# Four layers of a graph network: other buffers and another order at both ends of the program

## The chip, the core and the metric

The kernel runs on one core of a Trainium2 chip. The core has five engines that run their own instruction streams and wait for each other by semaphores: TensorE (PE, matrix products), VectorE (DVE), ScalarE (ACT), GpSimd (POOL) and SyncE (SP, which here only issues DMAs). The metric is the device time of one execution in microseconds (us); lower is better. Times are given as the median of several runs. A profile is one further execution, recorded instruction by instruction; its span is the time from the first to the last recorded instruction.

## What is computed

The input is 128 graphs of 128 nodes with 256 features, and one adjacency matrix for each. Four layers follow each other; every one adds its result to its input and normalises the sum over the features.

```python
x = layernorm(x + L0(x, adj, a0..a3))        # attention: scores (x * a_k) @ x.T picked by adj == k+1,
                                             # leaky_relu, softmax, @ x
x = layernorm(x + L1(x, adj, W_msg, W_upd))  # mean of the neighbours' messages, + x @ W_upd + bias, relu
x = layernorm(x + L2(x, adj, weight, w_ih, w_hh, b_ih, b_hh))
# L2: three times   m = h @ weight[i];  aggr = A.T @ m;  h = GRU(aggr, h)
#     r, z = sigmoid(...); n = tanh(i_n + r * h_n); h = (1 - z) * n + z * h
x = layernorm(x + L3(x, adj, W, a))          # Wh = x @ W; e_ij = leaky_relu(f_i + f_j), f from Wh @ a
                                             # masked softmax over j, @ Wh, elu
```

## The kernel before, in words

**Groups and stages.** Four graphs make a group; there are 32 groups, `NG`. For each group the program records the operations of `loading`, `layer0`, `layer1`, `gru` (three steps, step0 to step2) and `layer3`. Several groups are under way at a time: while one is in its GRU steps, the next ones load and run layers 0 and 1, and the previous one runs layer 3. The last group's layer 3 is done in two halves of two graphs.

**A planner sets the order.** Nothing is issued while a layer's function runs. The functions record operations; `spread` and `paced` (line 334) give each a nominal time, from the table `TIMES`, the distance of groups `PERIOD` (line 294) and corrections for the first six and the last six groups, `HEAD` and `TAIL`. At the end a loop goes through an estimate of the engines: at each turn it takes the engine that is free first, and of that engine's ready operations the one with the lowest nominal time. So the constants decide the order of each engine's stream, and a change of them moves instructions everywhere. The stream itself is fixed when the program is built; on the chip each engine runs its own in order. Every operation is recorded through one helper, so the profile gives line 229 for all of them; tiles tell them apart.

**Buffers.** `tile_of(tag, shape, bufs)` (line 136) asks for one of `bufs` buffers of that tag. A new tile of a tag has to wait until an old one of the same tag has been read for the last time. The tags that matter: `x_blocks`, `x_in`, `adj_in` (a group's input), `alpha0` (layer 0's scores), `xs`, `xT` (products' operands in layer 0), `x1T` (layer 0's result, turned), `rT` (the residual of the GRU layer, turned), `xc` (its result), `t_r`, `t_i`, `t_z`, `q` (parts of the gates), `e`, `alpha3`, `xd` (layer 3). PSUM has four banks named `ps` and four named `gate`.

**Turning a matrix.** [...]states are turned several times per group. The ordinary way is `turn` and `back`: DVE transposes blocks of 32x32 into `z`, SP writes `z` to DRAM (`way_...`) and reads it back in the other order with four DMAs. For the first group, and for the result of the last group's last step, `turned_quick` is used: PE transposes four blocks into a PSUM bank and ACT copies it out.

**The GRU step.** `sums` (line 735) forms four sums `t_h` of the state's quarters (on POOL) and four `t_m` of the aggregate (on DVE), so that each gate takes seven half products in place of eight. `gate` issues them in turn with evictions between. `update` (line 823) forms the new state in `hT`, turns it (`way_h`, `hn`), and `split` (on DVE) makes the three bf16 parts, `hn` and two `rest`, that the next step's aggregate needs as exact operands: products with `a_ne`. The next step's gates need the new `hT` only, the aggregate needs `hn` and `rest`.

**Layer 3.** `layer3` (line 883) computes the statistics of `xc`, products of `rT` with `w3x`, evicts them as `wh` scaled by the inverse deviation on ACT, and brings f_j of all nodes into every partition: DVE turns a column into `z_f`, SP writes it to DRAM (`way_f`) and reads it back broadcast into `e`. Then masks, softmax, products with `wh`, ELU (two ReLUs, Exp), the last `normalise` (line 538) and the store.

**Weights.** `weights` (line 370) loads them from ACT's and SP's queues, turns `w_ih`, `w_hh` and `weight` on PE, and multiplies `weight` by `w_ih` (the 24 products each with `wh,hT` and `xc,hT`) so that step i needs one matrix `c_gi`. It runs in the same planner beside the first groups' loads and layer 0.

Of the kernel before, what the change touches and what calls it, by code (L numbers as in the profile page):

```python
# [18 lines left out]
def kernel(  # L19
# [71 lines left out]
    class View:  # L91
# [38 lines left out]
        def real(self):  # L130
# [3 lines left out]
            return ap  # L134

    def tile_of(tag, shape, bufs=1, dtype=F32, pool=work):
        buf = Buf(pool, list(shape), dtype, tag, bufs)
        return View(buf, list(shape), [(0, n) for n in shape])
# [98 lines left out]
    PAIRS = ("tensor_tensor", "tensor_add", "tensor_sub", "tensor_mul", "scalar_tensor_tensor", "copy_predicated")  # L237
    SERVED = {"e": 3.5, "x1T": 0.9, "adj_in": 1.6, "x_in": 1.6, "xc": 1.5, "way_x2": 1.5, "way_f": 0.2}

# [43 lines left out]
    def sp_cost(op, n, out, ins, pointers, sums):  # L283
# [9 lines left out]

    PERIOD = 82.02493
    EAGER, RUSH = 5.3026, 1.3855
    HOP, PE_HOP, SLACK, DMA_SLACK = 0.0942, 0.0830, 0.2614, 0.8331
    STAGES = ("loading", "layer0", "layer1", "step0", "step1", "step2", "layer3")
    TIMES = {
        "loading": ((-247.5491, -194.0561), (-143.2722, -216.6135),),
        "layer0": ((-168.5251, -107.0951),),  # L300
        "layer1": ((-55.2002, 2.6695),),
        "step0": ((-4.9084, 19.3012), (-1.4435, 21.3222), (15.5190, 41.5941),),
        "step1": ((50.8640, 70.9820), (56.8513, 77.3906), (67.7313, 96.3666),),
        "step2": ((107.7073, 126.4989), (122.9713, 129.9877), (118.3791, 151.2368),),
        "layer3": ((179.8434, 241.7064),),
    }
    HEAD = (
        (-126.155, 5.128, -69.803, -21.348, -13.669, -8.174, -16.851),
        (80.207, 34.377, 38.524, -17.547, 20.300, -9.109, -5.064),
        (7.408, -12.202, 25.610, 5.632, -5.558, 8.108, 7.059),  # L310
        (-65.918, 41.138, 4.487, 5.072, -12.230, 11.065, -14.228),
        (-137.367, -1.144, -2.252, -1.129, -3.189, 2.308, 8.092),
        (153.242, -9.402, 11.531, 0.561, -10.941, 4.205, 0.017),
    )
    TAIL = (
        (27.368, -6.179, -9.810, -20.906, -9.678, 2.832, 10.136),
        (-37.995, 0.038, 5.644, -1.049, -11.456, -16.322, -4.360),
        (57.786, 10.690, 2.358, -3.167, -6.918, -6.271, -6.896),
        (-15.895, -28.941, -7.001, -17.741, -17.830, -3.775, -5.809),
        (-97.576, -12.624, -18.430, -10.462, 23.529, 14.526, 53.629),  # L320
        (97.074, 26.443, 18.854, 20.435, 13.060, 47.535, 73.872),
    )
# [11 lines left out]
    def paced(stage, part, g):  # L334

        start, end = TIMES[stage][part]
        at = g * PERIOD
        if g < len(HEAD):
            at += HEAD[g][STAGES.index(stage)]
        elif g >= NG - len(TAIL):  # L340
            at += TAIL[g - NG][STAGES.index(stage)]
        spread(at + start, at + end, stage[:4] == "step")

    def row(v, n):
# [25 lines left out]
    def weights():  # L370

        POOL.memset(neg_half, -0.5)
        nats, wnat = [], []
        for src, tag, bufs in ((w_ih, "hT", 9), (w_hh, "rest", 4)):
# [9 lines left out]
        spread(-215.1, -206.9)  # L384
        for k, a in enumerate((a0, a1, a2, a3)):
            SP.dma_start(out=acol[:, k, :], in_=a.rearrange("(c p) -> p c", p=P))
        spread(-182.0, -173.8)
        SP.dma_start(out=w_um[:, :, :D], in_=w_upd.rearrange("(c p) u -> p c u", p=P))
# [6 lines left out]
        SP.dma_start(out=arow, in_=row(a_att, 2 * D))  # L395
        spread(-165.5, -124.1)

# [7 lines left out]
        for n, dst in enumerate((w_ihT, [w_hhT[:, c] for c in range(KC)])):  # L405
            for g in range(NGC // 2):
                nat = nats[n * NGC // 2 + g]
                ps = bank()
                with PE:
                    for c in range(KC):  # L410
                        for e in range(2):
                            PE.transpose(
                                ps[:, (2 * c + e) * P : (2 * c + e + 1) * P], nat[:, e, c * P : (c + 1) * P], ident
                            )
                for c in range(KC):
                    out_of(dst[c][:, 2 * g * P : (2 * g + 2) * P], ps[:, 2 * c * P : 2 * (c + 1) * P])


        for i in range(NL):
            wT = tile_of("hT", [P, KC, D], 9)  # L420
            ps = bank()
# [7 lines left out]
            for d in range(KC):  # L429
                for n0, n1 in ((0, 512), (512, 3 * D)):  # L430
                    ps = bank()
                    with PE:
                        for e in range(KC):
                            PE.matmul(
                                ps[:, : n1 - n0],
                                wT[:, e, d * P : (d + 1) * P],
                                w_ihT[e][:, n0:n1],
                                start=(e == 0),
                                stop=(e == KC - 1),
                            )  # L440
                    out_of(c_gi[:, i, d, n0:n1], ps[:, : n1 - n0])


# [35 lines left out]
        for c in range(KC):  # L479
            DVE.tensor_sub(w3x[:, c, :], w3x[:, c, :], ps[:, : 2 + D])  # L480
        spread(-157.2, -16.5)

# [55 lines left out]
    def normalise(res, shift, rstd, quick):  # L538

        for b in range(res.shape[1]):  # L540
            if quick and b % 2 == 0:
                DVE.tensor_scalar(
# [51 lines left out]
    def layer0(g, s):  # L594
# [39 lines left out]
        for h in range(G // 2):  # L634
# [5 lines left out]
            for j in range(2):  # L640
# [4 lines left out]
                )  # L645
        normalise(res, *statistics(res, "0"), g == 0)
        s.x1T = tile_of("x1T", [P, G, KC, N])
# [11 lines left out]
    def layer1(g, s):  # L659
# [17 lines left out]
        for b in range(G):  # L677
# [14 lines left out]
        normalise(res, *statistics(res, "1"), g == 0)  # L692

        s.hT, s.parts, s.ways = [], [], []
        for c in range(KC):
            t = tile_of("hT", [P, T], 9)
# [12 lines left out]
    def gru(g, s):  # L709
# [5 lines left out]
        def step(i, hT, parts):  # L715
# [107 lines left out]
            def update(c, z, n, d):  # L823

                DVE.scalar_tensor_tensor(d, z, 1.0, d, op0=OP.add, op1=OP.mult)
                new[c] = n if last_step else tile_of("hT", [P, T], 9)
                DVE.scalar_tensor_tensor(new[c], d, 0.5, n, op0=OP.mult, op1=OP.add)
                if last_step:
                    turning[c] = s.x3[:, :, c * P : (c + 1) * P]
                else:  # L830
                    turning[c] = tile_of("hn", [P, G, P], 3)
                if last_step and g == NG - 1:
                    turned_quick(turning[c], [new[c][:, b * N : (b + 1) * N] for b in range(G)])
# [16 lines left out]
            if last_step:  # L850
# [32 lines left out]
    def layer3(g, s, first, last):  # L883
# [48 lines left out]
        pT, rinv = softmax(alpha, three, end, tile)  # L932
        normalise(x3, shift, rstd, end)

# [3 lines left out]
        for h in range(n // 2):  # L938
# [167 lines left out]
```

## Time and profile before

| | us |
|---|---|
| median of 3 runs | 2739.55 (2733.42 to 2739.82) |
| the profiled execution's own time | 2739.76 |
| its span | 2737.9 |
| PE busy with products | 2675.7 |
| DVE busy | 2207.6 |
| ACT busy | 1798.1 |
| POOL busy | 1619.3 |

The profile counts an engine as busy while one of its instructions runs. PE's weight loads are counted apart (PEld). An f32 product is two records, a bf16 product one. "PEclk" is the clock that PE was granted, as a share of full speed. Lines of the timeline read: start, duration, engine, operation, tiles written and read, count, and in brackets how long the engine was idle before and who released it.

### The profile page before, as it was taken

The numbers are of one execution on the slowest core, as the hardware profiler recorded it, in microseconds if no ns is written. First come the engines' busy times: TensorE is split into PE (matmuls) and PEld (weight loads), VectorE is DVE, ScalarE is ACT, GpSimd is POOL, SyncE is SP. The second block draws the span as 40 slices with busy tenths as digits, with TensorE's granted clock in tenths as the row PEclk, the third lists the DMA queues.
The fourth block names the chain that finished last, engine by engine and source line by source line (L and its number), as shares of the span: only waits on it lengthen the run. The fifth ranks groups of instructions, "written<-read, shape, count | busy, mean of one in ns | idle before, by whom it ended". The sixth has DMA issues, their size and how long they took to land.

```text
span 2737.9 us, 45131 instructions
## 1 busy us (share of the span) xinstructions
PE 2675.7 (98%) x14332; PEld 2232.2 (82%) x14332; DVE 2207.6 (81%) x5044; ACT 1798.1 (66%) x4336; POOL 1619.3 (59%) x1546
## 2 busy tenths in 40 slices
PE   8999999999999999999999999999999999999996
PEld 5788888788888888888888888888888888888784
DVE  5777788888788888888888788888888878888775
ACT  4557666666776666776666776666776666666665
POOL 4555656555666555666555667555656555666542
PEclk9999999999999999999999999999999999999997
DMA  5445555465555555555555555555555556553532
GB/s 121 102 80 116 96 118 115 91 120 103 111 110 111 106 119 100 113 111 110 108 117 106 107 111 110 110 115 108 105 113 108 106 104 117 100 110 81 104 70 51
DMA packets 1385662, 288.38 MB, mean 105 GB/s; under 512 B 1139408, under 2 KB 1385296, under 8 KB 1385424
## 3 DMA queue, kind: packets, MB, share of 16 engines
q1 hardware_dynamic: 1382976, 283.13, 52.1%
q10 hardware_dynamic: 2448, 2.36, 0.3%
q8 instruction: 115, 1.88, 0.3%
q14 instruction: 123, 1.01, 0.1%
HBM read 168.96 MB, written 116.38 MB: 104 GB/s over the span
## 4 chain that ended last, share of the span: by engine, by line
PE 84%; DVE 8%; ACT 4%; DMA 1%; issue 1%; SPq 1%; POOL 1%; DVEq 0%; POOLq 0%; ACTq 0%
PE gate L229 57%; PE ps L229 27%; DVE t_d L229 1%; DVE hT L229 1%; DVE z L229 1%; DVE t_m L229 1%; SPq L229 1%; DVE rest L229 1%; ACT xc L229 1%; ACT t_z L229 0%; ACT xs L229 0%; DVE t_z L229 0%; DVE xb L229 0%; DMA hn<-way_h 0%; ACT alpha L229 0%
## 5 line engine op out<-in xcount | busy, mean ns | idle before, releaser
L229 POOL TENSOR_TENSOR t_r<-t_r,t_i 128x512 f32<-128x512 f32 x186 | 248.7, 1349 | 242.4 <-DVE t_r L229 118.6
L229 PE MATMUL gate<-t_h,w_hhT 128*128 128x256 f32 x1152 | 343.5, 384 | 8.3 <-ACT t_z L229 6.7
L229 PE MATMUL gate<-t_h,w_sh 128*128 128x256 f32 x1152 | 338.4, 383 | 7.0 <-ACT q L229 4.0
L229 PE MATMUL gate<-t_m,c_gi 128*128 128x256 f32 x1152 | 341.4, 379 | 0.0
L229 PE MATMUL gate<-agT,c_gi 128*128 128x256 f32 x1152 | 338.8, 382 | 0.6 <-DVE q L229 0.3
L229 PE MATMUL gate<-t_m,w_sm 128*128 128x256 f32 x1152 | 339.1, 379 | 0.2 <-ACT t_i L229 0.2
L229 PE MATMUL gate<-hT,w_hhT 128*128 128x256 f32 x1152 | 333.0, 383 | 2.6 <-DVE mv L229 1.6
L229 POOL TENSOR_TENSOR t_d<-hT,t_n 128x512 f32<-128x512 f32 x192 | 257.4, 1349 | 43.3 <-ACT t_n L229 43.0
L229 PEld LDWEIGHTS gate<-t_h,w_sh 128*128 128x128 f32 x1152 | 210.2, 190 | 70.0 <-issue 18.4
L229 POOL MEMSET alpha<- 128x512 f32 x64 | 33.4, 522 | 392.7 <-DVE z L229 349.9
L229 PEld LDWEIGHTS ps<-xs,xT 128*128 128x128 f32 x2048 | 250.4, 194 | 11.5 <-ACT xs L229 2.5
L229 PE MATMUL ps<-xs,xT 128*128 128x128 f32 x2048 | 254.1, 278 | 3.2 <-DVE xa L229 1.4
L229 PEld LDWEIGHTS gate<-t_h,w_hhT 128*128 128x128 f32 x1152 | 207.1, 190 | 56.2 <-issue 16.3
L229 PEld LDWEIGHTS gate<-hT,w_hhT 128*128 128x128 f32 x1152 | 215.3, 191 | 43.4 <-issue 12.3
L229 POOL TENSOR_TENSOR rstd<-rstd,neg_half 128x4 f32<-128x4 f32 (+1 forms) x128 | 157.0, 1227 | 147.9 <-DVE rstd L229 147.0
L229 PEld LDWEIGHTS gate<-t_m,w_sm 128*128 128x128 f32 x1152 | 218.1, 190 | 32.2 <-issue 1.2
L229 PEld LDWEIGHTS gate<-agT,c_gi 128*128 128x128 f32 x1152 | 216.5, 190 | 32.3 <-DVE q L229 2.3
L229 PEld LDWEIGHTS gate<-t_m,c_gi 128*128 128x128 f32 x1152 | 217.3, 190 | 30.6 <-issue 0.7
L229 PE MATMUL ps<-w_um,x1T 128*128 128x512 f32 x512 | 240.6, 593 | 0.4 <-ACT x1T L229 0.2
L229 ACT ACTIVATE q<-gate,bhn 128x256 f32<-128x256 f32 x384 | 182.1, 474 | 83.8 <-PE gate L229 78.9
L229 POOL TENSOR_SCALAR mk<-a_f 128x512 uint8<-128x512 f32 x128 | 200.9, 1576 | 27.8 <-DVE alpha L229 18.5
L229 ACT COPY t_r<-gate 128x256 f32<-128x256 f32 x288 | 106.6, 370 | 153.8 <-PE gate L229 153.2
(185 smaller groups left out, 6746.3 us busy)
## 6 DMA issues: line engine op xcount, KB each, us to landing
way<-z SPq DMA_DIRECT2D x188, 256.0 KB, 2.5
way_h<-z SPq DMA_DIRECT2D x128, 256.0 KB, 2.4
hn<-way_h SPq DMA_DIRECT2D x512, 64.0 KB, 2.3
x_blocks<-in_x_dram SPq DMA_DIRECT2D x256, 64.0 KB, 2.4
x_in<-in_x_dram SPq DMA_DIRECT2D x32, 512.0 KB, 4.3
rT<-way SPq DMA_DIRECT2D x256, 64.0 KB, 2.3
way_p<-z SPq DMA_DIRECT2D x62, 256.0 KB, 2.5
probT<-way_p SPq DMA_DIRECT2D x248, 64.0 KB, 2.5
```

Of the source, the lines that this page charges most:

```text
L229: getattr(self.engine, name)(*[a.real() if isinstance(a, View) else a for a in args], **{k: a.real() if isinstance(a, View) else a for k, ...
```

## The change

Seven edits, and new constants for the planner:

- `lent`: for some groups a tag is replaced by another tag whose buffers are idle then. Group 1 takes its inputs and its layer 0 in buffers of layer 3 and of the gates. Groups 30 and 31 take `rT`, `xc`, `q`, `t_r`, `t_i` and `t_z` of the GRU in buffers of loads and of layers 0 and 1.
- The last group's new states after step1 too are turned by `turned_quick` (before: after step2 alone).
- `t_h` is formed on DVE in two steps: group 0's step0 and the last group's step2.
- In the last group's layer 3 DVE takes two of the four ReLUs of each half.
- The last `normalise` of group 30 goes to DVE as a whole.
- `way_f` is written as one row of 512 and read back as one.
- The weights' stages are given their times in seven parts by `early`, with constants of their own, so their loads and their work stand elsewhere among the first groups' operations. `hT` has 8 buffers instead of 9.

```diff
+    lent = {}
+
     def tile_of(tag, shape, bufs=1, dtype=F32, pool=work):
+        tag, bufs = lent.get(tag, (tag, bufs))
         buf = Buf(pool, list(shape), dtype, tag, bufs)
...
-    SERVED = {"e": 3.5, "x1T": 0.9, "adj_in": 1.6, "x_in": 1.6, "xc": 1.5, "way_x2": 1.5, "way_f": 0.2}
+    SERVED = {"e": 1.3, "x1T": 0.9, "adj_in": 1.6, "x_in": 1.6, "xc": 1.5, "way_x2": 1.5, "way_f": 0.2}
...
-    PERIOD = 82.02493
+    PERIOD = 81.73028
...
+        "weights": ((-80.6792, -53.8982), (-234.5413, -66.3537), (-85.3398, -177.0436), (-97.3878, -222.0278), (-90.3491, -54.1657), (-171.8955, -44.6841), (-116.1849, 18.7475),),
...
+    def early(part):
+
+        spread(*TIMES["weights"][part])
...
-            if quick and b % 2 == 0:
+            if b % 2 < quick:
...
-                if last_step and g == NG - 1:
+                if g == NG - 1 and i > 0:
                     turned_quick(turning[c], [new[c][:, b * N : (b + 1) * N] for b in range(G)])
...
-            of_h = sums(POOL, hT, w_hhT, w_sh, hT, "t_h")
+            of_h = sums(DVE if g + i in (0, NG + 1) else POOL, hT, w_hhT, w_sh, hT, "t_h")
...
-            way = tile_of("way_f", [P, 32], 4, F32, dram)
-            SP.dma_start(out=way, in_=z)
-            SP.dma_start(out=f, in_=way.rearrange("(m r) c -> r m c", [8, 16, 32], r=8)[0].partition_broadcast(P))
+            way = tile_of("way_f", [16, 32], 4, F32, dram)
+            SP.dma_start(out=way, in_=z.rearrange("(m r) c -> r m c", [8, 16, 32], r=8)[0])
+            SP.dma_start(out=f, in_=way.partition_broadcast(P))
...
-                ACT.activation(res[:, b, :], pb, AF.Relu, scale=rinv[:, b : b + 1])
-                ACT.activation(pb, pb, AF.Relu, scale=ninv[:, b : b + 1])
+                for to, by in ((res[:, b, :], rinv), (pb, ninv)):
+                    if end and j == 0:
+                        DVE.tensor_scalar(to, pb, by[:, b : b + 1], 0.0, op0=OP.mult, op1=OP.max)
+                    else:
+                        ACT.activation(to, pb, AF.Relu, scale=by[:, b : b + 1])
...
-        normalise(res, *statistics(res, three), end)
+        normalise(res, *statistics(res, three), 2 if g == NG - 2 else int(end))
...
+    LENT = {
+        1: {
+            "x_blocks": ("t_z", 1), "x_in": ("t_i", 1), "adj_in": ("alpha3", 1), "alpha0": ("e", 1),
+            "probT_0": ("probT_3", 1), "x1T": ("xd", 1), "xs": ("rT", 2),
+        },
+        NG - 2: {"xc": ("xa", 2), "rT": ("xT", 2)},
+        NG - 1: {
+            "q": ("x_in", 1), "t_r": ("x_blocks", 1), "t_i": ("xb", 2), "t_z": ("xb", 2),
+            "xc": ("xa", 2), "rT": ("xs", 2),
+        },
+    }
...
+        lent.update(LENT.get(g, {}) if g == 1 else {})
         loading(g, s)
         layer0(g, s)
...
+        lent.clear()
+        lent.update(LENT.get(g, {}) if g > 1 else {})
         gru(g, s)
```

The remaining lines of the diff are the other constants of `TIMES`, `HEAD` and `TAIL`, the calls of `early` in `weights`, and `int(...)` around the third argument of `normalise`. In PE's stream the change adds eight transposes of 128x128, all in group 31, and removes nothing; DVE's grows by 14 instructions, SP's loses ten DMAs. The order of the streams differs throughout: between groups 13 and 22 both kernels repeat one pattern of products per group, and the two patterns are not the same.

More of the change, by code (lines that the diff above doesn't have):

```diff
@@ L291 @@
     engines = (PE, DVE, ACT, POOL, SP)
-    PERIOD = 82.02493
-    EAGER, RUSH = 5.3026, 1.3855
-    HOP, PE_HOP, SLACK, DMA_SLACK = 0.0942, 0.0830, 0.2614, 0.8331
+    PERIOD = 81.73028
+    EAGER, RUSH = 4.9441, 1.5064
+    HOP, PE_HOP, SLACK, DMA_SLACK = 0.0975, 0.1022, 0.2622, 0.8243
     STAGES = ("loading", "layer0", "layer1", "step0", "step1", "step2", "layer3")
     TIMES = {
[L299 to L305, printed above, removed]
+        "weights": ((-80.6792, -53.8982), (-234.5413, -66.3537), (-85.3398, -177.0436), (-97.3878, -222.0278), (-90.3491, -54.1657), (-171.8955, -44.6841), (-116.1849, 18.7475),),
+        "loading": ((-270.5681, -253.3431), (-73.2168, -291.6634),),
+        "layer0": ((-167.8607, -107.2636),),
+        "layer1": ((-55.0836, 1.9826),),
+        "step0": ((-0.0120, 6.9518), (0.2402, 27.6105), (15.5871, 41.1624),),
+        "step1": ((50.3003, 61.9650), (57.0688, 76.7749), (63.5441, 96.9672),),
+        "step2": ((105.0974, 124.9583), (122.1936, 130.3892), (118.2271, 151.0122),),
+        "layer3": ((180.2686, 241.7351),),
@@ L306 @@
     }
     HEAD = (
[L308 to L313, printed above, removed]
+        (-8.812, -175.978, -47.271, -14.819, 0.990, 29.605, 4.780),
+        (9.303, 38.059, -27.415, 8.695, 4.650, -13.814, 31.463),
@@ L314 @@
+        (-161.158, -14.643, 11.133, 0.523, -1.844, 22.264, 10.467),
+        (-173.643, 45.499, 14.505, 11.786, 0.810, 10.190, -5.124),
+        (-171.750, -3.449, 12.137, -8.917, 5.023, 2.080, 7.957),
+        (-245.977, -21.192, 24.177, 5.969, 4.162, 11.377, 24.028),
     )
     TAIL = (
[L316 to L319, printed above, removed]
@@ L320 @@
-        (-97.576, -12.624, -18.430, -10.462, 23.529, 14.526, 53.629),
-        (97.074, 26.443, 18.854, 20.435, 13.060, 47.535, 73.872),
+        (127.197, -10.789, 1.076, -13.469, 10.703, 11.032, 13.210),
+        (17.815, -18.016, -1.019, -11.707, 1.115, -15.520, -14.882),
+        (80.227, -2.934, 25.075, -16.097, -14.182, 5.595, 38.386),
+        (92.761, -52.578, -27.642, -24.660, -19.396, -6.316, 54.637),
+        (216.288, -67.705, -36.885, -29.712, 25.798, 36.675, 75.653),
+        (364.741, 17.401, 10.112, 11.988, 17.448, 68.637, 12.013),
@@ L373, in weights @@
         nats, wnat = [], []
-        for src, tag, bufs in ((w_ih, "hT", 9), (w_hh, "rest", 4)):
+        for src, tag, bufs in ((w_ih, "hT", 8), (w_hh, "rest", 4)):
             for g in range(0, NGC, 2):
@@ L383, in weights @@
                     wnat.append(w)
-        spread(-215.1, -206.9)
+        early(0)
         for k, a in enumerate((a0, a1, a2, a3)):
             SP.dma_start(out=acol[:, k, :], in_=a.rearrange("(c p) -> p c", p=P))
-        spread(-182.0, -173.8)
+        early(1)
         SP.dma_start(out=w_um[:, :, :D], in_=w_upd.rearrange("(c p) u -> p c u", p=P))
@@ L395, in weights @@
         SP.dma_start(out=arow, in_=row(a_att, 2 * D))
-        spread(-165.5, -124.1)
+        early(2)
         evict = [DVE.tensor_copy, ACT.copy]
@@ L416, in weights @@
                     out_of(dst[c][:, 2 * g * P : (2 * g + 2) * P], ps[:, 2 * c * P : 2 * (c + 1) * P])
+            early(3 + n)
         for i in range(NL):
-            wT = tile_of("hT", [P, KC, D], 9)
+            wT = tile_of("hT", [P, KC, D], 8)
             ps = bank()
@@ L441, in weights @@
                     out_of(c_gi[:, i, d, n0:n1], ps[:, : n1 - n0])
+        early(5)
         for n in range(NL + 1):
@@ L480, in weights @@
             DVE.tensor_sub(w3x[:, c, :], w3x[:, c, :], ps[:, : 2 + D])
-        spread(-157.2, -16.5)
+        early(6)
     def turned(src, n, tag):
@@ L645, in layer0 @@
                 )
-        normalise(res, *statistics(res, "0"), g == 0)
+        normalise(res, *statistics(res, "0"), int(g == 0))
         s.x1T = tile_of("x1T", [P, G, KC, N])
@@ L691, in layer1 @@
                 DVE.scalar_tensor_tensor(res[:, two], res[:, two], 0.0, x1[:, two], op0=OP.max, op1=OP.add)
-        normalise(res, *statistics(res, "1"), g == 0)
+        normalise(res, *statistics(res, "1"), int(g == 0))
         s.hT, s.parts, s.ways = [], [], []
         for c in range(KC):
-            t = tile_of("hT", [P, T], 9)
+            t = tile_of("hT", [P, T], 8)
             cols = slice(c * P, (c + 1) * P)
@@ L825, in update @@
                 DVE.scalar_tensor_tensor(d, z, 1.0, d, op0=OP.add, op1=OP.mult)
-                new[c] = n if last_step else tile_of("hT", [P, T], 9)
+                new[c] = n if last_step else tile_of("hT", [P, T], 8)
                 DVE.scalar_tensor_tensor(new[c], d, 0.5, n, op0=OP.mult, op1=OP.add)
@@ L932, in layer3 @@
         pT, rinv = softmax(alpha, three, end, tile)
-        normalise(x3, shift, rstd, end)
+        normalise(x3, shift, rstd, int(end))
         res = tile("xd", [P, n, D])
```

## The prediction

> **What bounds the kernel now.** I read the page first: its span, and the busy times.
>
> ```profile
> span 2737.9 us, 45131 instructions
> ...
> PE 2675.7 (98%) x14332; PEld 2232.2 (82%) x14332; DVE 2207.6 (81%) x5044; ACT 1798.1 (66%) x4336; POOL 1619.3 (59%) x1546
> ```
>
> TensorE (PE) is the bound, but 98% hides what is left. The Trainium skill, "Trainium Kernel Development and Optimization", section Best Practices, says that matmul busy time is a poor measure of the distance to the bound because matmuls are pipelined. The trace agrees: counted as work, PE has less than it shows. In the chain of waits a run of gate products gives the spacing.
>
> ```profile
> 2631.06 10.81 PE gate L229 x50
> ```
>
> 10.81 / 50 = 0.216 us per record of 256 columns. In the same way the timeline gives 0.111 for f32 records of 128 columns, 0.429 for 512, 0.056 for bf16 of 128 and 0.108 for transposes. Times the counts: 8064 gate records x 0.216 = 1742, 2048 xs,xT = 227, 512 w_um = 220, 2304 with a_ne = 129, 1280 with hu, w3x and probT = 278, the weights 24: 2619 us after rounding. The span is 2737.9, so 119 us are slack. Windows show where.
>
> ```profile
> 0.00:25.00 25.00, 18.73 (x81) 12.64 (x82) 11.83 (x25) 7.90 (x16) 8.18 (x16) 1.00 1.00 212
> 25.00:50.00 25.00, 21.44 (x129) 17.68 (x128) 13.83 (x39) 11.30 (x24) 18.59 (x16) 0.93 0.29 63
> 50.00:75.00 25.00, 20.18 (x102) 13.59 (x101) 18.71 (x52) 12.72 (x29) 10.90 (x14) 0.98 0.29 57
> ...
> 1400.00:1500.00 100.00, 99.79 (x534) 82.58 (x533) 82.06 (x190) 66.08 (x164) 59.15 (x58) 1.00 0.53 104
> ...
> 2660.00:2680.00 20.00, 16.33 (x62) 11.99 (x61) 10.99 (x25) 8.24 (x19) 6.30 (x7) 0.87 0.60 99
> 2680.00:2700.00 20.00, 17.89 (x84) 14.34 (x83) 10.99 (x22) 10.66 (x32) 0.31 (x1) 0.79 0.18 35
> 2700.00:2720.00 20.00, 12.89 (x48) 8.92 (x48) 12.34 (x34) 12.65 (x29) 10.29 (x9) 0.90 0.13 31
> 2720.00:2738.00 18.00, 4.63 (x12) 3.07 (x12) 8.01 (x26) 9.17 (x27) 1.38 (x2) 0.59 0.12 40
> ```
>
> The columns to read are PE busy with its record count, and PEclk. Counting records in each stretch, the slack is 30.4 us up to 125, 17.6 from 125 to 700, 25.2 from 700 to 2561 (1.3 per 100 us, with PE busy 99.8%), and 45.8 after 2561, of which 39 after 2660. So the middle has little to give; head and tail have most. PEclk falls below 1 in both: half clock for stretches of 3.4 us and more (13.7 us from 2675).
>
> In the tail the timeline shows group 31's state going through DRAM between step 1 and step 2, and then ScalarE (ACT) as a queue.
>
> ```profile
> 2670.48 0.71 DVE L229 STREAM_TRANSPOSE z<-hT 128x512 f32<-128x512 f32 x1
> ...
> 2673.47 0.38 SPq L229 DMA_DIRECT2D way_h<-z  x1
> ...
> 2677.72 2.08 SPq L229 DMA_DIRECT2D hn<-way_h  x4
> ...
> 2685.35 1.17 PE L229 MATMUL gate<-hT,w_hhT 128*128 128x256 f32 x2
> ...
> 2715.94 2.08 ACT L229 ACTIVATE xd<-xd,shift,rstd 128x256 f32<-128x256 f32 x4 [1.41 <-DVE shift L229]
> ...
> 2717.92 0.82 ACT L229 ACTIVATE wh<-ps,rstd 128x258 f32<-128x258 f32 x2
> ...
> 2725.73 0.47 ACT L229 ACTIVATE xd<-ps,rinv 128x256 f32<-128x256 f32 x1 [1.48 <-PE ps L229]
> ...
> 2729.37 0.58 ACT L229 ACTIVATE ps<-ps 128x512 f32<-128x512 f32 x1
> ```
>
> And in the head the first products of layer 0 wait for the attention vectors acol, issued behind ten other loads.
>
> ```profile
> 11.74 3.24 SPq L229 DMA_DIRECT2D acol<-in_L_gnn_a_dram  x4
> ...
> 19.92 1.34 ACT L229 ACTIVATE xs<-xT,acol 128x512 f32<-128x512 f32 x2
> ...
> 22.25 1.95 PE L229 MATMUL ps<-xs,xT 128*128 128x128 f32 x16
> ```
>
> **What the skill says.** "TensorE: Matmul & The Clock Gate", Part 1, says that the array falls to half clock after an idle window of about 3.4 us and needs a busy one to return. The trace agrees, and shows that the window need not be empty: half clock follows 2670.6 to 2675, in which PE did 1.3 us of work. "DMA: Bandwidth & Descriptors", Specifications, gives 512 B as the smallest piece for full rate. The trace fits: e<-way_f (256 KB in 128 B runs) lands after 5.5 us, adj_in (256 KB in 512 B runs) after 2.8.
>
> **The change part by part**, against the profiled run (span 2737.9, its own time 2739.76; the median is 2739.55, 0.2 less).
>
> *Head.* In the changed order two acol loads stand right after adj_in. That moves their issue from 11.74 (behind x_in) to about 11.2, and, as important, less is queued: the first xs could come near 17.5 instead of 19.9. PE meets layer 0's first product after 8.2 us of weight work instead of 12.9. But acol 2 and 3 now stand behind group 1's nine loads (before: 4.6 us for eight), t_d and w3x: the last is issued near 25 and lands after 4.3 (acol's time), near 29. So the fourth product ends near 31, against 36.0. POOL masks would allow 28. From there to step 0 the chain (leaky, softmax, layer 0, layer 1; 36.0 to 78.9) is unchanged but for its fillers: gain 5, bounds 0 and 7. x_in of group 0 moves behind 37 other loads: issue near 31, landing 4.3 later, 35.5; needed near 38. If that cover (2.5 us) goes, PE waits one for one. Lent buffers let group 1's layer 0 begin without waiting for group 0's tiles; its 7 us of products fill the same softmax gap as before, so no more than 1 us is added from 75 to 125, where the slack is 7 (t_h of step 0 on DVE too: four 128x256 at 0.42 instead of about 0.73 on POOL). Sum 6.
>
> *f_j in one run.* e's readback goes from 2048 runs of 128 B to 128 of 2 KB, and the write before it from 16 KB to 2. Bound: adj_in's 2.8 instead of 5.5, 31 times, but layer 3 is never late in the middle: 0 on the path.
>
> *Middle.* All pace constants change, so the order does. PE's work grows by eight transposes, 0.86 us, all in group 31. With 25 us of slack over 1861 us the order cannot give much; from 125 to 700 it can give or take some 6 of 17.6. I take 0, bounds -8 and +10.
>
> *Before the last step, 2561 to 2669* (slack 6.6): lent buffers relieve rT and xc of groups 30 and 31, and 29's final normalise no longer stands as one block of four on ACT before t_z (1.14 us of PE wait at 2644). I take 1, bounds -2 and +3.
>
> *Group 31's states by TensorE.* Let T = 2668.7, the end of step 1's last product. Before: the second hT is ready at T+4.0, the aggregates end at 2685.6 (T+16.9), and the first gates after run at half clock until 2688.6, which costs 1.9 more. After: hT (the first at T+1.8) is transposed on PE behind two of group 30's w3x products, ACT copies it (0.59) between 30's wh (four at 0.4) and xa (0.6 each), about T+4.8 and T+6.6; DVE then runs z_f, four t_h (0.42) and four rest (0.7 each) in that order, ending at T+8.8. Aggregates end near T+9.1, with two step-0 products (0.9) still to do. (16.9 + 1.9) - (9.1 + 0.9) = 8.8. PE runs 5 of these 9 us, so I expect full clock; if not, 3 come back. I take 8, bounds 5 and 9. Removed with it: eight reads and two writes on SP; new on ACT: two copies with gate evictions queued behind, in the sum.
>
> *End of layer 3.* Both transposes of rT now stand before the w3x products instead of one after an eviction and two w3x: bn_stats began at 2714.56, 10.7 after the gates; the copies now end about 7.7 after, if 30's ACT work allows: 2.5, bounds 1 and 3.5. Group 30's four normalises (2.08 on ACT just ahead of wh) go to DVE: wh starts when rstd is there, 2717.3 for 2717.9, less 0.4 since one stands between copy_predicated and reduce: 0.3. ReLUs: ACT worked from 2725.73 to 2729.95; four of eight at about 0.46 go to DVE: 1, bounds 0.3 and 1.5.
>
> Sum: 6 + 0 + 1 + 8 + 2.5 + 0.3 + 1 = 18.8. 2739.8 - 18.8 = 2721.0 for the profiled run; for the median **2721**.
>
> **The rivals.** (1) *The head is bound by its loads.* For: DMA share 1.00 in the first 25 us, and group 0's x_in and w_um go behind two more groups' blocks. Against: bytes ahead of the last acol (4.4 MB) had landed by about 20 us before. Then 6 is lost: 2727. (2) *The tail is throttled anyway.* For: gaps remain at each hand-over. Against: more PE work in them. It and late copies cost 6: 2727. (3) *Slower: layer 0's turn through DRAM.* In groups 11 to 25 the new order leaves 24.3 us of PE work (mostly) between the last layer 0 product and the first layer 1 product; it was 64.9. Before, group 14's turn took from 1085.7 to 1110.8, 25.1 us. For: 25.1 is over 24.3. Against: nothing needed that x1T until 1150.5, so its steps lay waiting; group 2 did it in 19.5 (120.8 to 140.3). At 27 us each of 15 groups waits 2.4: 36, so 2757. It makes the kernel slower by 0.3% from a turn of 26.4 on. (4) *The new ripple eats it*: 10 us of new small waits in the middle and 3 less in the tail: 2734.
>
> **How the numbers follow.** Forecast 0.62; (1) 0.14; (2) 0.10; (3) 0.05; (4) 0.09. What counts as no change is 0.3%, 8.2 us: 2731.3 to 2747.8. Forecast, (1) and (2) are faster, less 0.02 for their edges: 0.84; (4) and edges 0.10; (3) and edges 0.06. Bounds summed with care give 2710 at the low end; 2735 takes in (1), (2) and half of (4).
>
> **What would show it.** Right: first xs,xT near 17 to 18 us, step 0 of group 0 before 75; windows in the middle at 99.8%; from step 1's last product of group 31 to step 2's first t_m some 9 to 10 us, PEclk near 1 around 2660 to 2680; no ACT xd block of 2.08 before wh. Wrong: PE waiting for DVE/ACT hu after x1T in most groups; a PE wait for x_in near 36; a half clock right after step 1 of group 31.

## The result, and the profile after

| | before | after |
|---|---|---|
| median, us (5 runs each) | 2739.82 (2733.42 to 2741.08) | 2713.78 (2713.55 to 2717.58) |
| ratio | 1 | 0.9912, 95% interval 0.9897 to 0.9926 |
| span of the profiled execution | 2737.9 | 2711.9 |

The changed kernel is faster by 0.9%: 26.0 us in the medians and 26.0 in the spans. The page of the changed kernel:

```profile
span 2711.9 us, 45196 instructions
...
PE 2663.1 (98%) x14340; PEld 2232.4 (82%) x14340; DVE 2187.9 (81%) x5058; ACT 1806.7 (67%) x4330; POOL 1596.5 (59%) x1538
```

PE's busy time fell by 12.6 us although PE has eight transposes more to do. So busy time held some waiting, as the prediction took it to. I count slack as there: time less the sum of records times their spacing; time at half clock counts as slack too. It says where the 26.0 us come from. T is the end of group 31's last product of step 1 (2668.8 before, 2655.5 after), G the end of its last gate product.

| stretch | slack before | slack after | gain | term of the prediction |
|---|---|---|---|---|
| up to 125 us | 30.4 | 25.7 | 4.7 | 6 |
| 125 to 700 | 17.6 | 14.4 | 3.2 | 0 |
| 700 to 2561 | 25.2 | 21.6 | 3.5 | 0 |
| 2561 to T | | | 1.9 | 1 |
| T to G | 35.1 long | 26.9 long | 8.1 | 8 |
| G to the end | 34.1 long | 29.4 long | 4.6 | 3.8 |

Windows of the changed kernel; the columns are PE, weight loads, DVE, ACT and POOL busy with their record counts, then PEclk, the DMA share and GB/s:

```profile
0.00:25.00 25.00, 18.64 (x97) 14.52 (x98) 10.56 (x24) 9.61 (x19) 10.49 (x19) 1.00 0.93 195
25.00:50.00 25.00, 23.69 (x137) 17.49 (x135) 16.52 (x42) 11.78 (x25) 17.58 (x16) 1.00 0.39 107
50.00:75.00 25.00, 19.80 (x89) 13.80 (x89) 19.05 (x57) 10.28 (x26) 11.78 (x13) 0.93 0.38 79
...
1400.00:1500.00 100.00, 100.00 (x540) 83.89 (x539) 85.63 (x202) 66.76 (x166) 56.38 (x57) 1.00 0.53 110
...
2660.00:2680.00 20.00, 17.78 (x98) 14.92 (x96) 13.76 (x26) 12.97 (x36) 2.72 (x3) 1.00 0.17 40
2680.00:2700.00 20.00, 13.18 (x53) 9.55 (x54) 13.31 (x45) 13.07 (x37) 8.30 (x8) 0.91 0.08 28
2700.00:2711.90 11.90, 0.88 (x4) 0.42 (x3) 7.40 (x22) 3.91 (x8) 1.38 (x2) 0.64 0.13 45
```

Against the windows of before: DMA is a little less full in the first 25 us (0.93 for 1.00), PE does more from 25 to 50 (23.69 for 21.44) and still has a gap from 50 to 75. From 1400 to 1500 it is busy without a break (99.79 before). PEclk is 1.00 in 2660 to 2680, where it was 0.87; the last stretch is still at 0.64 (before: 0.59). In the timeline of the changed kernel's tail (start, duration, engine, operation, idle before):

```profile
2657.93 0.63 PE L232 MATMUL ps<-ident,hT 128*128 128x128 f32 x4 [0.66 <-DVE hT L232]
...
2659.11 0.60 ACT L232 COPY hn<-ps 128x512 f32<-128x512 f32 x1
...
2663.53 0.28 PE L232 MATMUL ps<-a_ne,rest 128*128 128x128 bf16 x2
...
2664.23 0.59 PE L232 MATMUL gate<-hT,w_hhT 128*128 128x256 f32 x2
```

Each new hT is transposed by PE at once and ACT's copy follows. The last product of the aggregates (the last with `a_ne`) ends at 2663.8, T + 8.3, and from there gate products follow each other on PE. Before, the state went through DRAM and the aggregates ended at T + 16.8. Next comes the end of layer 3:

```profile
2690.55 0.84 ACT L232 ACTIVATE wh<-ps,rstd 128x258 f32<-128x258 f32 x2 [1.56 <-POOL rstd L232]
...
2693.81 1.06 DVE L232 TENSOR_SCALAR xd<-xd,rstd,shift 128x256 f32<-128x256 f32 x3
...
2694.78 0.44 DVE L232 COPY_PREDICATED alpha<-m_gt,e 128x256 f32<-128x256 uint8 x1
...
2696.53 0.77 PE L232 MATMUL ps<-ident,alpha 128*128 128x128 f32 x2 [3.42 <-ACT alpha L232]
...
2697.89 2.06 PE L232 MATMUL ps<-wh,probT 128*128 128x256 f32 x4
...
2699.75 1.13 PE L232 MATMUL ps<-x_in,probT 128*128 128x256 f32 x4
```

wh now starts 8.1 us after G (2682.5); before, it was 14.0. ACT is free by then: no block of 2.08 us stands ahead of wh any more, group 30's four normalises are on DVE. But copy_predicated stands behind three of them. It starts 4.2 us after wh, where it was 2.6 before (wh at 2717.92):

```profile
2720.49 0.45 DVE L229 COPY_PREDICATED alpha<-m_gt,e 128x256 f32<-128x256 uint8 x1 [1.87 <-ACT e L229]
```

PE then waits 3.4 us for alpha and does the four records of wh,probT in 2.06 us, about half its rate; before, they took 2.07.

### The profile page after: what moved, and what is told of

It is laid out like the page before. It is cut to its first block, busy times and chain, and to the rows that moved or that the text cites. A ratio compares the mean times of both kernels' runs of the same rounds, so it can differ in the third digit from the quotient of the medians.

```text
span 2711.9 us, 45196 instructions
## 1 busy us (share of the span) xinstructions
PE 2663.1 (98%) x14340; PEld 2232.4 (82%) x14340; DVE 2187.9 (81%) x5058; ACT 1806.7 (67%) x4330; POOL 1596.5 (59%) x1538
## 4 chain that ended last, share of the span: by engine, by line
PE 85%; DVE 9%; ACT 2%; DMA 2%; issue 1%; SPq 1%; POOL 0%; POOLq 0%; DVEq 0%; ACTq 0%
PE gate L232 58%; PE ps L232 27%; DVE z L232 1%; DVE xb L232 1%; DVE st L232 1%; DVE t_d L232 1%; SPq L232 1%; DVE rest L232 1%; DMA e<-way_f 1%; DVE t_m L232 1%; DVE t_r L232 0%; DVE xa L232 0%; DVE hT L232 0%; DMA hn<-way_h 0%; DVE t_z L232 0%
## 5 line engine op out<-in xcount | busy, mean ns | idle before, releaser
L232 POOL TENSOR_TENSOR rstd<-rstd,neg_half 128x4 f32<-128x4 f32 x128 | 147.7, 1154 | 197.6 <-DVE rstd L232 124.7
L232 PEld LDWEIGHTS gate<-t_h,w_hhT 128*128 128x128 f32 x1152 | 208.9, 190 | 60.4 <-issue 23.2
L232 PEld LDWEIGHTS gate<-t_h,w_sh 128*128 128x128 f32 x1152 | 212.3, 190 | 54.3 <-issue 16.7
L232 PEld LDWEIGHTS ps<-xs,xT 128*128 128x128 f32 x1984 | 242.0, 193 | 12.5 <-issue 2.2
L232 PE MATMUL ps<-xs,xT 128*128 128x128 f32 x1984 | 244.2, 276 | 2.6 <-DVE xa L232 1.4
L232 PEld LDWEIGHTS gate<-t_m,w_sm 128*128 128x128 f32 x1152 | 217.1, 190 | 34.1 <-DVE t_m L232 2.2
L232 PEld LDWEIGHTS gate<-agT,c_gi 128*128 128x128 f32 x1152 | 216.8, 190 | 31.8 <-ACT t_r L232 1.2
L232 PEld LDWEIGHTS gate<-t_m,c_gi 128*128 128x128 f32 x1152 | 218.0, 190 | 30.2 <-ACT t_i L232 0.2
L232 PEld LDWEIGHTS gate<-hT,w_hhT 128*128 128x128 f32 x1152 | 214.2, 190 | 30.8 <-issue 2.9
L232 PE MATMUL ps<-w_um,x1T 128*128 128x512 f32 x496 | 232.7, 593 | 1.1 <-ACT x1T L232 1.1
L232 POOL TENSOR_SCALAR mk<-a_f 128x512 uint8<-128x512 f32 x128 | 212.3, 1665 | 20.7 <-DVE alpha L232 13.2
L232 POOL MEMSET alpha<- 128x512 f32 (+1 forms) x63 | 33.1, 525 | 314.0 <-DVE z L232 277.8
L232 ACT ACTIVATE xs<-xT,acol 128x512 f32<-128x512 f32 x248 | 173.2, 719 | 41.2 <-PE ps L232 30.6
```

The lines of the kernel that those rows point to most:

```text
L232: getattr(self.engine, name)(*[a.real() if isinstance(a, View) else a for a in args], **{k: a.real() if isinstance(a, View) else a for k, ...
```

## The experiments

All twelve against the kernel before, with the ratio's 95% interval. "After" is the changed kernel; a row's name says which kernel the run starts from and what it changes. "Middle" is the slack from 125 to 2561 us. Of six profiles whose orders differ from the changed kernel's at most in the head and in the last stages (after, e4, e6, e7, e8, e12) the middle is 33.7 to 36.2, of before and e2 42.8 and 43.4: read differences of 2.5 us as none.

| kernel | median, us | ratio | slack to 125 | middle | T to G | G to end |
|---|---|---|---|---|---|---|
| before | 2739.8 | 1 | 30.4 | 42.8 | 35.1 | 34.1 |
| after | 2713.8 | 0.9912 (0.9897 to 0.9926) | 25.7 | 36.0 | 26.9 | 29.4 |
| e1 after, f_j old | 2739.8 | 1.0006 (0.9998 to 1.0015) | 25.9 | 57.9 | 27.4 | 30.2 |
| e2 before, f_j new | 2740.0 | 1.0004 (0.9996 to 1.0012) | 31.4 | 43.4 | 34.8 | 34.0 |
| e3 code, constants of before | 2759.1 | 1.0074 (1.0062 to 1.0087) | 26.5 | 72.6 | 25.3 | 33.5 |
| e4 after, group 31 by DMA | 2726.4 | 0.9954 (0.9941 to 0.9966) | 26.6 | 36.2 | 36.6 | 31.8 |
| e5 f_j old, planner told | 2747.0 | 1.0031 (1.0020 to 1.0042) | 25.4 | 56.9 | 28.8 | 33.5 |
| e6 after, end plain | 2714.5 | 0.9911 (0.9897 to 0.9924) | 25.2 | 33.9 | 26.9 | 30.8 |
| e7 acol first | 2716.0 | 0.9915 (0.9902 to 0.9929) | 27.5 | 34.3 | 26.9 | 29.7 |
| e8 e7, normalise on POOL | 2714.7 | 0.9914 (0.9901 to 0.9928) | 27.3 | 33.7 | 26.9 | 29.4 |
| e9 f_j new, order of e5 | 2747.4 | 1.0030 (1.0018 to 1.0041) | 25.8 | 57.5 | 28.8 | 32.8 |
| e10 four lent tags undone | 2715.9 | 0.9915 (0.9900 to 0.9931) | 26.4 | 34.7 | 26.9 | 30.2 |
| e11 before, weights' times | 2743.2 | 1.0017 (1.0010 to 1.0023) | 27.5 | 50.1 | 33.8 | 34.1 |
| e12 after, t_h on POOL | 2712.8 | 0.9905 (0.9892 to 0.9919) | 25.3 | 33.9 | 26.3 | 29.8 |

### The middle: f_j's readback and the order (e1, e2, e5, e9, e3)

e1 is the changed kernel with these lines of before, and with the constants left, so that no engine's order changes:

```diff
-            way = tile_of("way_f", [16, 32], 4, F32, dram)
-            SP.dma_start(out=way, in_=z.rearrange("(m r) c -> r m c", [8, 16, 32], r=8)[0])
-            SP.dma_start(out=f, in_=way.partition_broadcast(P))
+            way = tile_of("way_f", [P, 32], 4, F32, dram)
+            SP.dma_start(out=way, in_=z)
+            SP.dma_start(out=f, in_=way.rearrange("(m r) c -> r m c", [8, 16, 32], r=8)[0].partition_broadcast(P))
```

> The changed kernel with f_j written and read back as before (16 KB written, 2048 runs of 128 B read back), every engine's order otherwise as in the changed kernel. Theory: the readback is off the path, so the 6.7 us gained between 125 and 2561 us come from the order; span within 1.5 us of the changed kernel's 2711.9, ratio to the kernel before about 0.991. Rival: the middle's gain is the relief of the DMA queues; then 4 to 7 us come back, span 2716 to 2719, ratio about 0.993, and PE's slack between 125 and 2561 goes from 36 back towards 43.

Both theories missed: the old readback costs the whole gain, 26 us, and 21.9 of them as slack in the middle. e2 is the same edit the other way round on the kernel before, whose order it keeps.

> The kernel before with only f_j's readback in one run, every engine's order as in the kernel before. Theory: nothing, ratio 1.000 and span 2737.9 within 1.5 us. Rival (relief of the DMA queues gives the middle): 4 to 7 us less, ratio about 0.998, slack between 125 and 2561 near 37 instead of 43.

Nothing, as the theory had it: 43.4 for 42.8. So a relief of the queues alone gives nothing, and the readback is worth 0 in one order and 26 us in the other. The traces show why. The issues of e1, then of the changed kernel (KB each, median us from issue to landing; the write before it, `way_f<-z_f`, lands after 2.0 us in both):

```profile
e<-way_f SPq DMA_DIRECT2D x31, 256.0 KB, 5.5
```

```profile
e<-way_f SPq DMA_DIRECT2D x31, 256.0 KB, 3.9
```

The timeline of e1 in one group, and the same instructions in the changed kernel:

```profile
1493.97 0.44 SPq L232 DMA_DIRECT2D e<-way_f  x1
...
1499.52 0.99 ACT L232 ACTIVATE e<-e,wh 128x128 f32<-128x128 f32 x3 [1.76 <-DMA e<-way_f]
...
1500.66 0.47 ACT L232 ACTIVATE q<-gate,bhn 128x256 f32<-128x256 f32 x1
...
1501.19 0.70 PE L232 MATMUL gate<-t_h,w_sh 128*128 128x256 f32 x2 [1.06 <-ACT q L232]
```

```profile
1480.81 0.44 SPq L232 DMA_DIRECT2D e<-way_f  x1
...
1484.81 0.99 ACT L232 ACTIVATE e<-e,wh 128x128 f32<-128x128 f32 x3 [0.20 <-DMA e<-way_f]
...
1485.96 0.46 ACT L232 ACTIVATE q<-gate,bhn 128x256 f32<-128x256 f32 x1
...
1486.83 0.65 PE L232 MATMUL gate<-t_h,w_sh 128*128 128x256 f32 x2
```

In the changed kernel ACT comes to e 3.8 us after the load's issue, waits 0.20 us and starts at 4.00 (1480.81 to 1484.81); PE doesn't wait. With the old readback ACT stands until 5.55 us after issue (1499.52), and the eviction q, next but one behind it, is 1.06 us too late for PE's gate products. ACT's waits for e from 700 to 2561 (total, times, longest) in e1, in the changed kernel and before:

```profile
ACT e L232 <- DMA e<-way_f: 29.8, 20, 4.2
...
ACT e L232 <- DMA e<-way_f: 7.0, 7, 2.1
...
ACT e L229 <- DMA e<-way_f: 7.6, 10, 1.9
```

So ACT waited for e in the kernel before too. In e2 these waits are gone and PE gains nothing: there they were not on PE's path. The two orders ask for e at different times: in e2, where ACT never waits for it, ACT starts on e a median 5.3 us after the issue, in the changed kernel 4.2. The old landing time of 5.5 nearly fits the first and is too long for the second.

From the changed kernel to e1, PE's listed waits in the middle rise from 9.1 to 20.0 us, of which those for ACT's q from 0.5 (2 times) to 7.1 (14 times). That is half of the 21.9. Another 1.7 is a stretch of half clock of 3.4 us at 430 us, which the changed kernel doesn't have; the rest is spread over spacings that the list of waits doesn't name.

e5 tells the planner so, by the one number that stands for e's landing; e9 keeps the order of e5 and takes the new readback.

```diff
-    SERVED = {"e": 1.3, ...
+    SERVED = {"e": 3.5, ...
```

> The changed kernel with f_j written and read back as before, and the planner told so (SERVED of e 3.5 in place of 1.3), so that ACT's first instruction on e may be put later. Theory: the 26 us that the old readback cost in the changed order come from ACT waiting for e with gate evictions behind it; an order that knows the landing time gives most of them back: 2714 to 2722 us, ACT's waits for e<-way_f between 700 and 2561 near 7 us instead of 29.8. Rival: the constants of the changed kernel fit no other landing time; then it stays at 2732 or more.

> The changed kernel with the new readback of f_j, but the planner told the old landing time (3.5): every engine's order is that of the kernel that was told and had the old readback (2747.0). Theory: that one was slow by its order, since ACT waited little for e in it; so this stays near 2745, slack between 125 and 2561 near 55 instead of 36. Rival: it was slow by the readback; then 2714 to 2722.

In e5 ACT's waits for e are down to 4.0 us, as the theory asked, and the kernel is slower still, as its rival had it. e9 gives the same time with the quick readback. So that order is slow in itself, by 21 us in the middle, whatever the readback. PE's two longest listed waits in it, from 125 to 2561 (total, times, longest):

```profile
PE ps L232 <- ACT wh L232: 7.8, 5, 2.8
PE gate L232 <- ACT t_z L232: 6.3, 12, 1.1
```

They are evictions on ACT again, but not the same ones as in e1. e3 has all edits of the code and every constant of before; the weights' work has the one stretch of before:

```diff
-    PERIOD = 81.73028
-    EAGER, RUSH = 4.9441, 1.5064
+    PERIOD = 82.02493
+    EAGER, RUSH = 5.3026, 1.3855
...
```

> All edits of the code, with the planner's constants of the kernel before (the weights' times too). Theory: head and middle come from the constants, the tail from the code: slack up to 125 stays near 30, from 125 to 2561 near 43, and the stretch from group 31's last step-1 product to its last gate product falls from 35 to about 27; sum about 8 to 10 us less than before, 2730, ratio 0.9965. Rival: the lent buffers and the other code edits give head and middle too: 2720 or less, ratio 0.993 or less.

Its tail came about as the theory had it (T to G from 35 to 25, for 27), its middle did not: 72.6 instead of 43, with ACT waiting 16.7 us for e though it has the quick readback. What of the edits moved that order so (8 hT buffers for 9, e at 1.3, the lent tags) was not separated. Of three orders made with the quick readback from nearly the same code, the middle is 36.0, 57.5 and 72.6. So the middle depends on how the constants fit the code, and the 42.8 of before could be undercut.

### The tail (e4, e6, e8, e12)

e4 turns group 31's states after step 1 through DRAM again, with the planner free to place what follows:

```diff
-                if g == NG - 1 and i > 0:
+                if last_step and g == NG - 1:
```

> The changed kernel with group 31's states after step 1 turned through DRAM again. Theory: these are worth 8 us: the stretch from group 31's last step-1 product to its last gate product goes from 27 back to 35, span 2720, ratio 0.994, and half clock comes back after step 1. Rival: the order of the tail and the full clock give part of the 8 whatever the way of turning; then the stretch is 29 to 32 and the span 2714 to 2717.

It lost 13.1 us of span (12.6 in the medians), more than either theory. 9.6 are in the stretch from T to G, 2.4 after G and 1.1 before T. The timeline of e4 (T is 2656.6):

```profile
2658.89 0.71 DVE L232 STREAM_TRANSPOSE z<-hT 128x512 f32<-128x512 f32 x1
...
2665.19 2.53 SPq L232 DMA_DIRECT2D hn<-way_h  x4
...
2671.03 0.27 PE L232 MATMUL ps<-a_ne,hn 128*128 128x128 bf16 x1 [1.72 <-DMA hn<-way_h]
...
2674.04 1.17 PE L232 MATMUL gate<-hT,w_hhT 128*128 128x256 f32 x2
```

The second hn lands 14.4 us after T, and gate products after it run at half rate (1.17 us for two records, 0.59 in the changed kernel; PEclk is 0.50 from 2672 to 2676). The 2.4 us after G follow from it: group 30's layer 3 comes later and stands between group 31's last updates on DVE, so PE waits 3.19 and 2.52 us for the two xs that it turns; in the changed kernel 0.45 and 0.74. So one edit carries both the 8 of the prediction and much of its 3.8.

e6 takes the ReLUs and group 30's normalise back to ACT.

```diff
-                    if end and j == 0:
+                    if False:
...
-        normalise(res, *statistics(res, three), 2 if g == NG - 2 else int(end))
+        normalise(res, *statistics(res, three), int(end))
```

> The changed kernel with all ReLUs of the last layer 3 on ACT and group 30's last normalise on ACT, as before; PE's order is the same. Theory: the two edits are worth 1.3 us together, span 2713.2. Rival: DVE's four normalises stand ahead of copy_predicated and the reduce on the path, and cost what the ReLUs give; span 2711 to 2712. Neither shows in the ratio, 0.991.

G to end is 30.8 for 29.4, the 1.4 that the theory had; but four kernels with the end of the changed one show 29.4 to 30.2, and some of the 1.4 is PE's clock. The four records of x_in,probT took 1.91 us in e6 and in e10, 1.13 in the changed kernel: half clock lasted longer. Between 0.6 and 1.4 us, then; the span moved by only 0.3 because T came 1.1 earlier. The two edits pull against each other, as the rival said: in e6 copy_predicated starts 11.3 us after G, in the changed kernel 12.3, so the normalises on DVE cost 1.0 there, and the ReLUs give more than that back.

e8 moves group 30's normalises to POOL, off the path, with e7's loads:

```diff
+            if quick == 2:
+                POOL.tensor_scalar(
+                    res[:, b, :], res[:, b, :], rstd[:, b : b + 1], shift[:, b : b + 1],
+                    op0=OP.mult, op1=OP.add,
+                )
-            if b % 2 < quick:
+            elif b % 2 < quick:
...
-            "xc": ("xa", 2), "rT": ("xs", 2),
+            "xc": ("xa", 2), "rT": ("xs", 2), "xd": ("rT", 2),
```

> The kernel with acol first, and group 30's last normalise moved from DVE to POOL, which idles there, with group 31's first result in a buffer of rT so that it doesn't wait for that store. Theory: copy_predicated then starts when the second e is there, 1.0 us earlier, and the reduce 1.4 earlier; end 1.0 to 1.4 less than with acol first alone, so about 2708 to 2711. Rival: POOL's instructions slow DVE's beside them, or the second half's chain on ACT sets the end; then nothing.

The reduce did start 12.0 us after G for 13.2 in e7, and the end came only 0.3 nearer to G. PE in e8:

```profile
2696.29 0.62 PE L232 MATMUL ps<-ident,alpha 128*128 128x128 f32 x2 [2.23 <-ACT alpha L232]
...
2698.08 2.08 PE L232 MATMUL ps<-wh,probT 128*128 128x256 f32 x4
2699.95 1.72 PE L232 MATMUL ps<-x_in,probT 128*128 128x256 f32 x4
```

Half clock lasts 3.4 us in both kernels. In e7 it ends at 2701.7, soon after the last four records have started at 2701.5; in e8 it covers most of them, and they take 1.72 us for 1.14. The second copy_predicated, beside POOL's normalise, took 0.69 us for 0.43. What the path gained was given back in those two places.

e12 forms t_h on POOL in both steps, as before.

```diff
-            of_h = sums(DVE if g + i in (0, NG + 1) else POOL, hT, w_hhT, w_sh, hT, "t_h")
+            of_h = sums(POOL, hT, w_hhT, w_sh, hT, "t_h")
```

> The changed kernel with t_h on POOL in group 0's step 0 and group 31's step 2, as before; PE's order differs only there. My step: four sums of 0.42 us on DVE for 0.73 on POOL, so 1 us at most in each place: step 1 of group 0 up to 1 us later, gates of the last step up to 1.2 later; span 2712 to 2714. Rival: the sums on POOL free DVE for rest and agT, and nothing or a gain shows.

No loss: the aggregates end at T + 9.4 for 8.3, and the gates still end 0.6 us nearer to T. No gain from the edit shows. e12 has the lowest median of all, 1 us below the changed kernel, which the intervals don't tell apart. I have no version that is shown to beat the changed kernel.

### The head (e7, e10, e11, and e3)

e7 gives the acol loads, the second part of the weights, an earlier time, so that all four stand behind adj_in:

```diff
-        "weights": ((-80.6792, -53.8982), (-234.5413, -66.3537), ...
+        "weights": ((-80.6792, -53.8982), (-262.0, -261.0), ...
```

> The changed kernel with all four loads of acol right behind adj_in; PE's order is the same. Theory: the fourth attention vector came late, so layer 0's last product ends near 29 instead of 33.9, and step 0 of group 0 starts 2 to 3 us before 75.1; span 2709 to 2710. Rival: the last loads land in time already (the fourth was issued at 20.8), and the chain is held by the masks on POOL and by weight products ahead on PE; then step 0 starts at 75 and the span is 2711 to 2712.5.

The rival's mechanism was right, though step 0 started at 76.8 and the span was 2713.6, both later than it had them. SP issues the four at 10.6 to 12.5, and yet the first stretch of xs,xT starts at 18.69 (17.88 in the changed kernel, where weight products ahead of it ran at full rate earlier) and the fourth ends at 35.6 (33.8). PE between them:

```profile
27.49 1.95 PE L232 MATMUL ps<-xs,xT 128*128 128x128 f32 x16
29.27 1.02 PE L232 MATMUL ps<-wh,hT 128*128 128x512 f32 x2
30.13 1.02 PE L232 MATMUL ps<-xc,hT 128*128 128x512 f32 x2
31.83 1.12 PE L232 MATMUL ps<-wh,hT 128*128 128x512 f32 x2 [0.68 <-ACT c_gi L232]
32.79 1.02 PE L232 MATMUL ps<-xc,hT 128*128 128x512 f32 x2
33.65 1.95 PE L232 MATMUL ps<-xs,xT 128*128 128x128 f32 x16
```

The fourth stretch, one for each attention vector, stands behind 512-wide weight products; the loads don't hold it.

e10 keeps only the inputs of group 1 lent; e11 is the kernel before with the changed kernel's seven times of the weights (the second diff shows two of the calls).

```diff
-            "x_blocks": ("t_z", 1), "x_in": ("t_i", 1), "adj_in": ("alpha3", 1), "alpha0": ("e", 1),
-            "probT_0": ("probT_3", 1), "x1T": ("xd", 1), "xs": ("rT", 2),
+            "x_blocks": ("t_z", 1), "x_in": ("t_i", 1), "adj_in": ("alpha3", 1),
```

```diff
-        spread(-215.1, -206.9)
+        early(0)
...
-        spread(-182.0, -173.8)
+        early(1)
```

> The changed kernel with four of group 1's seven lent tags undone (alpha0, probT_0, x1T and xs; the inputs stay lent). My step gave the lent buffers of group 1 at most 1 us and the order of loads and weights 5: then step 0 of group 0 still starts near 75.1. Rival, after the kernel with the code alone, in which it started at 72.5 with the loads of before: the lent buffers carry the head, and it goes back to 78 or 79, the slack up to 125 from 25.7 to about 30. The whole time may move by some us more either way, since the order after the head changes too.

> The kernel before with the changed kernel's times for the weights' seven parts and nothing else, no buffer lent. My step: the order of loads and weights gives 5 us at the head, step 0 of group 0 at 74. Rival (the lent buffers carry the head): step 0 at 77.5 to 79, slack up to 125 near 30.

Step 0 of group 0 starts at 75.5 in e10 (75.1 in the changed kernel) and at 74.6 in e11 (78.9 before): the order of loads and weights gives 4.3 us at that point without any lent buffer. But e3, with the weights as before and all edits of the code, the lent buffers among them, starts it at 72.5: there group 1's products rT,xT stand in the gap in which PE had waited 2.7 us for alpha. The slack up to 125 is 27.5 in e11, 26.5 in e3, and with both 25.7. So each way gives 3 to 4 us alone, and both together 4.7: they fill in part the same gaps. e11 also shows the other side of such an edit: 50.1 in the middle for 42.8.

## Why the prediction was right, and where not

The forecast of 2721 was 7 us too high; 2713.8 is inside the range, in its lower part. Of the 7.2 us, 6.7 are the middle; the head gave 1.3 less than forecast and the three terms of the tail together 1.8 more.

- **Group 31's states by TensorE** (8): the stretch shortened by 8.1, aggregates ended at T + 8.3 for a forecast of 9.1, PEclk was 1.00. Mechanism and size were right. Undone alone (e4) it is 13.1 us, 9.6 of them in this stretch, since half clock comes back, and 2.4 at the end of layer 3.
- **End of layer 3** (3.8): 4.6. The transposes ahead of w3x gave more than 2.5: bn_stats starts 5.4 us after G for 10.7. It was partly given back: from wh to the end it took 21.3 us for 20.0. The loss stands between wh and copy_predicated (4.2 us for 2.6), and group 30's normalises on DVE are 1.0 of it (e6). Half clock is no part of it: the kernel before did wh,probT at half clock too. The prediction charged the normalises 0.4. ReLUs and normalise together were forecast at 1.3; e6 leaves 0.6 to 1.4.
- **Head** (6): 4.7. The size was near and one reason wrong. I made acol's last load set the fourth product (issue near 25, end near 31); it was issued at 20.8, the product ended at 33.8, and PE's weight products stood before it; with all four loads issued by 12.5 (e7) it was no earlier. x_in was issued at 28.1, and no wait for it shows. And the two parts, 5 and 1, are not additive.
- **Before the last step** (1): 1.9.
- **Middle** (0, bounds -8 and +10): this term was mis-sized. It gained 6.7 us by the two profiles, 6.6 to 9.7 by the six of this order against the two of before's. PE's listed waits there fell from 13.7 us in 35 times to 9.1 in 22, those for ACT's t_z and q from 9.3 to 2.2. The reason given, that so little slack cannot give much, failed: about a sixth of it went. The gain lies within the upper bound; the lower one was too narrow for what an order can do: in e5, e9 and e3 nearly the same code has 14 to 30 us more slack there than before.
- **f_j** (0): right for the order of before (e2), wrong for the one that was built on it (e1). "Layer 3 is never late in the middle" did not hold even for ACT before, which waited 7.6 us for e; it held for PE. The new order asks for e about 1 us sooner and so needs the quick readback: without it the time is 2739.8, outside the range. That a term of 0 did no harm to the total is luck.
- The rivals: (1) the acol loads did not bind the head (e7). (2) The clock came back from T to G, not at the end, where PE was at half clock for 3.4 us from 2696.5. (3) No PE wait for hu shows in the steady groups: group 14's turn of layer 0 took 19.4 us (1083.2 to 1102.6), and PE had 23.2 us of other work meanwhile. The sum of this rival was off: 27 less 24.3 is 2.7 us and not 2.4, so some 40 us and 2761, with 0.3% reached from a turn of 26.1 on. (4) In this order the middle's slack fell; it rose by 14 to 30 us in e5, e9 and e3.

What stays open is which instructions of the new order make the middle better; the runs show that it takes both the order and the quick readback.

## What to carry to other kernels

Here a planner orders the streams, and a faster transfer was worth nothing in the old order and 26 us in one that was built on it. Price such a transfer together with the order, and look at the distance from its issue to its first reader. An engine that waits for it also holds the evictions queued behind it, so a stage that looks off the path can reach PE through ACT's queue: it did in e1, and not in the kernel before. And a middle with PE busy 99.8% can still hold a quarter of a change's gain, or lose more than the whole of it (e3).

## What was not expected of the hardware

- e<-way_f, 256 KB: 5.5 us with runs of 128 B, 3.9 with runs of 2 KB, where adj_in (512 B) takes 3.0. "DMA: Bandwidth & Descriptors", Specifications, in the Trainium skill names 512 B as the smallest piece for full rate; the trace agrees in direction, but the runs of 2 KB, read as a broadcast, took longer than adj_in: I had taken its 2.8 of the kernel before as the bound. Why was not tested.
- In the changed kernel half clock followed a PE wait of 3.42 us, as "TensorE: Matmul & The Clock Gate", Part 1, of the Trainium skill has it. In e8 the longest wait was 2.23 us, but PE worked only 1.2 us from 2694 to 2698, and half clock came at 2698 all the same. The window need not be empty, as the kernel before had shown already at 2675.
- The length of that half clock differs between executions with the same order at the end: it lasted 3.4 us in the changed kernel (from 2696.5) and to the end of the program in e10 (from 2696.6). So four records of x_in,probT took 1.13 to 1.91 us, which is 0.8 us of scatter in a span that ends there.
